# An LSTM with a residual: cutting the input product at whole products, and the order of small jobs at its head

## The chip, the cores and the metric

The kernel runs on one core of a Trainium2 chip. The metric is the time of one execution in device microseconds (us). A core has five engines that matter here. TensorE (PE) multiplies matrices into PSUM; VectorE (DVE) and ScalarE (ACT) do elementwise work; GpSimd (POOL) does a little of it; SyncE (SP) issues most of the transfers (DMAs). Each engine takes its own instructions in the order in which the program wrote them, and waits for others by semaphores. ACT and POOL can issue DMAs too, and then an issue stands in the same queue as their other work.

## What is computed

x has 32 sequences of 512 steps with 512 features, and the result is x plus the hidden states of an LSTM that runs over x:

```python
xW = jnp.einsum('ntd,dg->ntg', x, Wx) + b          # (32, 512, 2048)
def step(carry, xw_t):
    prev_h, prev_c = carry
    a = xw_t + prev_h @ Wh                          # Wh: 512 x 2048
    i = jax.nn.sigmoid(a[:, :Hd])
    f = jax.nn.sigmoid(a[:, Hd:2 * Hd])
    o = jax.nn.sigmoid(a[:, 2 * Hd:3 * Hd])
    g = jnp.tanh(a[:, 3 * Hd:])
    next_c = f * prev_c + i * g
    next_h = o * jnp.tanh(next_c)
    return ((next_h, next_c), next_h)
return x + swapaxes(hs, 0, 1)                       # hs: the 512 hidden states
```

All of it is float32. The product with Wh is serial: step t + 1 needs the hidden state of step t. The product with Wx depends on nothing in the loop, and can be done at any time before its step.

## The kernel before

**Column groups.** A batch of 32 fills 32 of PE's 128 columns. So each product is written as four matmuls, one for each quarter (q or j = 0 to 3) of the output's 128 partitions, and these run in PE's four column groups at the same time. "h" is the product of the hidden state with Wh: 16 matmuls of 512 columns in each step (four for each of four slices k), made by `h_part` (line 201, the matmul is line 210). "x" is the product with Wx. Each matmul shows as two records in the profile, with a weight load for each.

**The x product.** For steps 24 to 503 it is done in 20 groups of 24 steps by a bilinear scheme: 20 slots for each group, of 7 products each (r = 1 to 7), a product being four matmuls of 256 columns on line 477. A group has thus 140 products, 560 matmuls. Its left factors are sums of pieces of x, made by DVE on line 388 (`u_op`) from pair sums (lines 444 to 450) of what `load_group` (line 434) loads. Its right factors are rows of `vring`, loaded by `load_v` (line 556) from a DRAM table `vdram`, three rows ahead. The results are evicted from PSUM by ACT (lines 523, 532, 539) and DVE (lines 529, 533, 536) in `evacuate`, summed by DVE in `w_op` (line 353, 1024 columns), stored to DRAM (line 369), and loaded again by step (`load_xw`, lines 568 and 574).

**One step.** `h_part(t)` is written first, then the stores, loads and elementwise jobs, then the x matmuls (`emit_matmuls`), then `cell(t)`. So the x matmuls fill PE while the cell turns the gates into the next hidden state: ACT's sigmoids and tanh (lines 225 to 227), DVE's products (229, 230), tanh (232), the product with the output gate (234) and two transposes into `ht` (236). On DVE and ACT the jobs of step t stand ahead of `cell(t)`. `seed_step(t + 1)` (line 585) copies the x part of step t + 1 into the PSUM bank onto which `h_part(t + 1)` accumulates. POOL adds x to h for the output (line 244), and SP stores it (line 248).

**How many x matmuls a step gets.** The position `pos` counts x matmuls. In steps from `STREAM0` = 20 on, a step runs up to a target that grows by 560 / 24 = 23.33 matmuls:

```python
target = min(R * 7 * 4 + (t + 1 - STREAM0) * R * 7 * 4 // GS, 4 * len(items))
n = max(0, target - pos[0])
```

Steps thus get 23 or 24 matmuls, and most end inside a product.

**The head, steps 0 to 19.** The x product of the first 24 steps is done plainly (`plain_block`, line 159): five of them before step 0, nineteen in steps 0 to 9, which `keep` (line 715) evicts and stores to DRAM (`kept`, line 716). Meanwhile DVE makes the table of right factors (`v_add`, line 627), and ACT issues its stores (`v_store`, line 639, called by `flush_v`). From step 10 to 19 the stream of group 0 runs, 57 to 59 matmuls in a step (37 in step 19), in chunks of at most 24. After `cell(10)`, ACT issues three loads of bias rows (line 690); `late_seeds` (lines 694 to 704, DVE) makes from them, in step 11, banks' seeds that line 507 copies later. When the plain products and the jobs are over, at the end of step 9, `load_group(1)` is written on SP.

**The tail.** From step 478 on nothing is left of x but eight plain steps, and h alone runs.

Of the kernel before, what the change touches and what calls it, by code (L numbers as in the profile page):

```python
# [23 lines left out]
HEAD = 24  # L24
GS = 24
NG = 20
TAIL = T - HEAD - NG * GS
R = 20
TAU = (1, 0, 2)
NS = NG * R  # L30
KEPT = 5
AHEAD = 28
STREAM0 = HEAD + GS - AHEAD
# [32 lines left out]
PROD = 4 * 108.0  # L66
# [22 lines left out]
def kernel(  # L89
# [10 lines left out]
    nc = tc.nc  # L100
# [35 lines left out]
    def load_x(c, a=0, b=TC):  # L136
        nc.sync.dma_start(
            out=xnat[:, xslot(c), a:b].rearrange("p t q b -> p (t q b)"), in_=x[c][:, a * P : b * P]
        )
# [48 lines left out]
    def is_split(t):  # L188
        return t >= SPLIT

    def bank_of(t):
        if t < KEPT:
            return [gbank[0], gbank[1], xbank[3], xbank[4], xbank[0]][t]
        return gbank[t % 2]

    def half_of(t, i):
        if is_split(t):
            return PAIRS[t % 2][i][:, 0:HW]
        return bank_of(t)[:, i * HW : (i + 1) * HW]
# [234 lines left out]
    def load_group(g):  # L434
        nc.sync.dma_start(
            out=xs[g % 2][:, :, 0:4],
            in_=xg[g].rearrange("p (k s m) -> p k s m", k=6, s=4),
        )
# [14 lines left out]
    items = []  # L453
# [4 lines left out]
    pos = [0]  # L458
# [119 lines left out]
    def seed_step(t):  # L578

        src = xw_late[t] if t in xw_late else xw[:, t % 3]  # L580
        if is_split(t):
            for i in range(2):
                nc.scalar.copy(half_of(t, i), src[:, i * HW : (i + 1) * HW])
        else:
            nc.scalar.copy(bank_of(t), src)  # L585
# [94 lines left out]
    def flush_v():  # L680
        for f in v_stores:
            f()
        v_stores.clear()
# [4 lines left out]
    def load_seeds(pairs, queue):  # L688
        for i, j in pairs:
            queue.dma_start(out=seeds[i], in_=bias[j : j + 1].to_broadcast([P, W]))  # L690
# [21 lines left out]
    def keep(p):  # L712
        n = p - KEPT
        dst = parks[n % 6]
        add(dst, park_banks[n % 3], bias_full)
        kept_stores.append(lambda: nc.sync.dma_start(out=kept[n], in_=dst))

    with tc.manual_schedule():
# [37 lines left out]
        jobs = {}  # L756
# [3 lines left out]
        dve_jobs = []  # L760
# [4 lines left out]
        done_work = 0.0  # L765
        n_plain = 0
        group_loaded = 1
# [9 lines left out]
        for t in range(T):  # L777
            h_part(t)
            for f in stores + kept_stores:
                f()  # L780
            stores.clear()
            kept_stores.clear()
            store_blocks()
            c, rest = divmod(t + 6, TC)
            if rest == 0 and 3 <= c < NCHUNK - 1:
                load_x(c)
            if t == SPLIT - 4:
                load_x(NCHUNK - 1)
            if t == 3:
                load_x(2)  # L790
            if t == 5:
                load_seeds(((4, 3), (5, 1)), nc.sync)
                load_group(0)
            if t + 3 >= KEPT and t + 3 < HEAD + NG * GS and t >= 2:
                if t == 2:
                    pass
                load_xw(t + 3)

            if t < HEAD_STEPS:
                target = head_work * (t + 1) / HEAD_STEPS  # L800
                chunks = []
                while done_work < target - 200 and n_plain < HEAD - KEPT:
                    chunks.append(("plain", KEPT + n_plain))
                    n_plain += 1
                    done_work += PLAIN
                n = int((target - done_work) / PROD * 4 + 0.5) if n_plain == HEAD - KEPT else 0
                if t == HEAD_STEPS - 1 and n:
                    n = R * 7 * 4 - pos[0]
                left = n
                while left > 0:  # L810
                    m = min(left, 24)
                    chunks.append(("stream", m))
                    left -= m
                done_work += n * PROD / 4
                todo = jobs.pop(t, [])
                plains = sum(k == "plain" for k, _ in chunks)
                for i, (kind, m) in enumerate(chunks):
                    if kind == "plain":
                        bank = park_banks[(m - KEPT) % 3]
                        room["dve"] = 3000.0  # L820
                        for cc in range(4):
                            plain_block(m, cc, bank)
                        if i == 0:
                            cell(t)
                            flush_v()
                        keep(m)
                        if m == HEAD - 1:
                            plains_done = t
                        last = i == plains - 1
                        for _ in range(len(todo) if last else -(-len(todo) // (plains - i))):  # L830
                            todo.pop(0)()
                    else:
                        load_v_ahead()
                        u_ahead(m)
                        room["dve"] = m * PROD / 4 * 1.5
                        evacuate()
                        if late_seeds_due and plains_done < t - 1:
                            late_seeds_due.pop()()
                        if t >= HEAD_STEPS - 3 and dve_jobs:
                            dve_jobs.pop(0)()  # L840
                        u_ahead(m + 24)
                        while wqueue and room["dve"] > 0:
                            w_op()
                        seed_banks(m)
                        emit_matmuls(m)
                        if i == 0:
                            cell(t)
                            flush_v()
                            if t == plains_done + 1:
                                load_seeds(((0, 0), (1, 1), (2, 2)), nc.scalar)  # L850
                if t + 1 >= KEPT:
                    seed_step(t + 1)
                if t >= 9 and not v_stores:
                    load_v_ahead()
                if group_loaded == 1 and n_plain == HEAD - KEPT and not dve_jobs and not jobs:
                    assert not v_stores
                    load_group(1)
                    group_loaded = 2
                    dve_jobs += [lambda i=i: pair_sum(1, i) for i in range(4)]
                continue  # L860

            target = min(R * 7 * 4 + (t + 1 - STREAM0) * R * 7 * 4 // GS, 4 * len(items))
            n = max(0, target - pos[0])
            after = max(0, min(R * 7 * 4 + (t + 2 - STREAM0) * R * 7 * 4 // GS, 4 * len(items)) - pos[0])
            room["dve"] = 3800.0 + min(0.0, room["dve"])
            evacuate()
            seed_banks(n)
            if t + 1 < T:  # L870
                seed_step(t + 1)
            load_v_ahead()
            u_ahead(after)
            g_now = items[min(pos[0] // 4, len(items) - 1)][0] // R
            if group_loaded < NG and pos[0] >= 28 * (R * (group_loaded - 1) + 4):
                load_group(group_loaded)
                s_done[group_loaded] = 0
                group_loaded += 1
            g = group_loaded - 1
            if s_done.get(g, 4) < 4 and pos[0] >= 28 * (R * (g - 1) + 9) and room["dve"] > 900:  # L880
                pair_sum(g, s_done[g])
                s_done[g] += 1
            while wqueue and room["dve"] > 300:
                w_op()
            if t == SPLIT - 9:
                late_weights[0] = True
            if t >= SPLIT - 9 and late_loads:
                late_loads.pop(0)()
            emit_matmuls(n)
            kept_late = []  # L890
            for _ in range(0 if t < SPLIT - 2 else 2 if t < SPLIT else 1):
                if plain_tail:
                    p, c = plain_tail.pop(0)
                    plain_block(HEAD + NG * GS + p, c, tail_banks[p % 2])
                    if c == 3:
                        kept_late.append(p)
            cell(t)
            for p in kept_late:
                dst = cbuf[:, take(free_c), 0:2].rearrange("p s c -> p (s c)")
                xw_late[HEAD + NG * GS + p] = dst  # L900
                add(dst, tail_banks[p % 2], bias_full)
            if t == T - 8:
                nc.vector.transpose(x_last, x_of(T - 1).rearrange("p q b -> p (q b)"))
# [50 lines left out]
```

## Time and profile before

| | us |
|---|---|
| median of 3 runs | 3174.75 |
| lowest, highest | 3170.27, 3176.18 |
| the profiled execution's own time | 3174.11 |
| its span, first to last instruction | 3172.0 |
| PE busy on h, L210, into gbank (16288 records) | 1885.6 |
| PE busy on x, L477, into xbank from ubuf (14400 records) | 1209.5 |
| DVE on L353 (480 of 1217 ns) | 580.6 |
| DVE waiting for the gates of ACT (L229 after L226) | 677.3 |
| ACT waiting for h (L225 after L210) | 1283.7 |
| mean granted TensorE clock, share of full | 0.997 |

The profile is of one execution. Busy time counts an engine as busy while at least one of its instructions runs; the matmuls of four column groups overlap, so a busy PE may be a quarter full. A timeline row gives start, duration, engine, line, operation, output and inputs with their shapes, the number of instructions, and in brackets the idle time before the first of them with what ended it. Rows with a q behind the engine (ACTq, SPq) are DMA issues. L585 is line 585 of the kernel before; in the kernel after, the lines from 825 on stand one or two lines further down.

### The profile page before, as it was taken

How to read it: one execution, taken by the hardware profiler on the slowest of the kernel's cores; microseconds unless marked ns; L12 is line 12 of the kernel's file. 1: busy time of each engine (PE TensorE's matmuls, PEld its weight loads, DVE VectorE, ACT ScalarE, POOL GpSimd, SP SyncE). 2: the span in 40 equal slices, each digit the busy share in tenths (PEclk: the TensorE clock that was granted, in tenths of full speed). 3: DMA queues.
4: the chain of work that ended last, by engine and by line, in shares of the span. 5: the costliest groups of instructions: out<-in, count | busy, mean ns of one | idle time of the engine just before them, and what ended most of it. 6: DMA issues, size and time to landing. Idle time of an engine off the chain costs nothing. (4 is left out here: it accounts for less than half of the span.)

```text
span 3172.0 us, 105017 instructions
## 1 busy us (share of the span) xinstructions
PE 3127.2 (99%) x41944; PEld 1999.5 (63%) x41944; DVE 2230.0 (70%) x6217; ACT 1453.0 (46%) x5481; POOL 232.9 (7%) x508
## 2 busy tenths in 40 slices
PE   9899999999999999999999999999999999999998
PEld 6445666666666666666666666666666666666565
DVE  5577767777776777677776767776777767677644
ACT  1144444444444444444444444444444444444444
POOL 0000000000000000000000000000000000000000
PEclk9899999999999999999999999999999999999999
DMA  8877777778778777877778777778777777777831
GB/s 288 291 252 254 249 255 247 249 239 257 254 234 264 227 257 242 262 239 252 243 251 264 226 259 238 255 248 257 241 246 250 252 260 228 251 245 237 269 97 38
DMA packets 311000, 766.66 MB, mean 242 GB/s; under 512 B 49392, under 2 KB 92144, under 8 KB 310000
## 3 DMA queue, kind: packets, MB, share of 16 engines
q1 hardware_dynamic: 296800, 740.82, 72.0%
q10 hardware_dynamic: 13712, 19.14, 1.7%
q8 instruction: 331, 5.42, 0.7%
q14 instruction: 157, 1.29, 0.1%
HBM read 577.04 MB, written 182.71 MB: 240 GB/s over the span
## 5 line engine op out<-in xcount | busy, mean ns | idle before, releaser
L210 PE MATMUL gbank<-wh_sb,ht 128*32 128x512 f32 (+1 forms) x16288 | 1885.6, 580 | 20.1 <-ACT gbank L585 5.5
L210 PEld LDWEIGHTS gbank<-wh_sb,ht 128*32 128x32 f32 x16288 | 843.4, 110 | 684.0 <-issue 311.1
L477 PE MATMUL xbank<-vring,ubuf 128*32 128x256 f32 x14400 | 1209.5, 379 | 8.7 <-DVE cbuf L533 5.2
L477 PEld LDWEIGHTS xbank<-vring,ubuf 128*32 128x32 f32 x14400 | 734.7, 110 | 261.9 <-issue 35.8
L225 ACT ACTIVATE s<-gbank 128x128 f32<-128x128 f32 x984 | 276.3, 281 | 1307.9 <-PE gbank L210 1283.7
L229 DVE TENSOR_TENSOR prod<-s 128x128 f32<-128x128 f32 x1024 | 293.2, 286 | 679.0 <-ACT s L226 677.3
L353 DVE TENSOR_TENSOR cbuf<-cbuf 128x1024 f32<-128x1024 f32 x480 | 580.6, 1217 | 3.3
L244 POOL TENSOR_TENSOR oc<-xnat,ht 128x128 f32<-128x128 f32 x504 | 232.7, 462 | 2901.5 <-DVE ht L236 1603.3
L232 ACT ACTIVATE tanh_c<-s 128x64 f32<-128x64 f32 x1024 | 262.2, 256 | 264.3 <-DVE s L230 260.4
L477 PE MATMUL bbank<-vring,ubuf 128*32 128x256 f32 x2400 | 306.6, 380 | 1.6 <-DVE cbuf L529 1.5
L236 DVE STREAM_TRANSPOSE ht<-hbuf 128x64 f32<-128x64 f32 x1022 | 250.9, 245 | 75.9 <-DVE hbuf L234 2.8
L585 ACT COPY gbank<-xw 128x512 f32<-128x512 f32 x473 | 284.8, 602 | 20.9 <-issue 8.4
L230 DVE TENSOR_TENSOR s<-prod 128x64 f32<-128x64 f32 x1024 | 230.3, 225 | 35.2
L523 ACT COPY cbuf<-xbank 128x512 f32<-128x512 f32 x400 | 233.3, 583 | 44.7 <-PE xbank L477 33.8
L477 PE MATMUL xbank<-vring,r 128*32 128x256 f32 x2400 | 247.5, 379 | 0.4 <-ACT xbank L507 0.4
L477 PE MATMUL xbank<-vring,xs 128*32 128x256 f32 x2400 | 241.8, 381 | 3.3 <-DMA vring<-vdram 3.3
L234 DVE TENSOR_TENSOR hbuf<-o,tanh_c 128x64 f32<-128x64 f32 x1024 | 211.9, 207 | 26.0 <-ACT tanh_c L232 25.4
L226 ACT ACTIVATE s<-gbank 128x64 f32<-128x64 f32 x984 | 228.2, 232 | 0.0
L533 DVE TENSOR_TENSOR cbuf<-xbank,cbuf 128x256 f32<-128x256 f32 x400 | 163.6, 409 | 79.3 <-ACT cbuf L532 76.8
L477 PEld LDWEIGHTS bbank<-vring,ubuf 128*32 128x32 f32 x2400 | 141.7, 110 | 57.1 <-issue 30.0
L529 DVE TENSOR_TENSOR cbuf<-bbank,cbuf 128x256 f32<-128x256 f32 x400 | 161.8, 405 | 4.3 <-PE bbank L477 4.3
L536 DVE TENSOR_TENSOR cbuf<-xbank,cbuf 128x256 f32<-128x256 f32 x400 | 162.3, 406 | 0.4 <-PE xbank L477 0.4
(83 smaller groups left out, 1778.6 us busy)
## 6 DMA issues: line engine op xcount, KB each, us to landing
vring<-vdram SPq DMA_DIRECT2D x340, 896.0 KB, 5.9
xwd<-cbuf SPq DMA_DIRECT2D x240, 512.0 KB, 6.4
xw<-xwd SPq DMA_DIRECT2D x1920, 64.0 KB, 3.6
out_dram<-oc SPq DMA_DIRECT2D x255, 128.0 KB, 2.9
xnat<-in_x_dram SPq DMA_DIRECT2D x63, 512.0 KB, 5.2
xs<-in_x_grouped_dram SPq DMA_DIRECT2D x10, 1536.0 KB, 10.3
vring<-vdram SPq DMA_DIRECT2D x20, 768.0 KB, 6.0
r<-in_x_grouped_dram SPq DMA_DIRECT2D x10, 1536.0 KB, 10.6
```

The lines of the kernel that those rows point to most:

```text
L210: nc.tensor.matmul(dst[j * B : (j + 1) * B], state["ht"][:, k], m, start=False, stop=True, skip_group_check=True)
L225: nc.scalar.activation(s[:, u, 0:2], g[:, n_, 0:2], AF.Sigmoid)
L226: nc.scalar.activation(s[:, u, 2], g[:, n_, 3], AF.Tanh)
L229: nc.vector.tensor_mul(prod[:, u], s[:, u, 0:2], s[:, u, 2:4])
L230: add(nxt[:, u, 3], prod[:, u, 0], prod[:, u, 1])
L232: nc.scalar.activation(tanh_c[:, HALVES[u]], nxt[:, u, 3], AF.Tanh)
L236: nc.vector.transpose(ht[:, 2 * u : 2 * u + 2].rearrange("p q b -> p (q b)"), hbuf[:, HALVES[u]])
L244: (nc.gpsimd if t < T - 8 else nc.vector).tensor_add(oc[:, tt % 2], x_of(t), ht)
L353: op(c_of(dst), c_of(src), c_of(bb))
L477: nc.tensor.matmul(dst[q * B : (q + 1) * B], left_of(gr, s, r)[:, q * B : (q + 1) * B], vring[:, row % 3, RIGHT[r]], start=start, stop=Tru ...
L523: nc.scalar.copy(t[:, 0:4:3], xb.rearrange("p (n c) -> p n c", n=2))
L585: nc.scalar.copy(bank_of(t), src)
```

## The change

Three things change, all in the order of the program; no arithmetic does.

1. The number of x matmuls in a step is rounded to a multiple of four, in the head (to the nearest) and in the stream (the target is rounded down to a whole product). In the stream the steps get 20 or 24 matmuls, one in six 20.
2. In the head `seed_step(t + 1)` moves from the end of the step to directly behind `cell(t)`, ahead of `flush_v`: on ACT the copy of line 585 then precedes the DMA issues of line 639 and the evictions of the later chunks.
3. The three bias loads of step 10 are issued by GpSimd in place of ScalarE, and `load_group(1)` waits for the end of step 13.

```diff
-                n = int((target - done_work) / PROD * 4 + 0.5) if n_plain == HEAD - KEPT else 0
+                n = 4 * int((target - done_work) / PROD + 0.5) if n_plain == HEAD - KEPT else 0
...
                         if i == 0:
                             cell(t)
+                            if t + 1 >= KEPT:
+                                seed_step(t + 1)
                             flush_v()
                         keep(m)
...
                         if i == 0:
                             cell(t)
+                            seed_step(t + 1)
                             flush_v()
                             if t == plains_done + 1:
-                                load_seeds(((0, 0), (1, 1), (2, 2)), nc.scalar)
-                if t + 1 >= KEPT:
-                    seed_step(t + 1)
+                                load_seeds(((0, 0), (1, 1), (2, 2)), nc.gpsimd)
                 if t >= 9 and not v_stores:
                     load_v_ahead()
-                if group_loaded == 1 and n_plain == HEAD - KEPT and not dve_jobs and not jobs:
+                if t >= 13 and group_loaded == 1 and n_plain == HEAD - KEPT and not dve_jobs and not jobs:
                     assert not v_stores
                     load_group(1)
...
-            target = min(R * 7 * 4 + (t + 1 - STREAM0) * R * 7 * 4 // GS, 4 * len(items))
+            target = min(R * 7 * 4 + (t + 1 - STREAM0) * R * 7 // GS * 4, 4 * len(items))
             n = max(0, target - pos[0])
-            after = max(0, min(R * 7 * 4 + (t + 2 - STREAM0) * R * 7 * 4 // GS, 4 * len(items)) - pos[0])
+            after = max(0, min(R * 7 * 4 + (t + 2 - STREAM0) * R * 7 // GS * 4, 4 * len(items)) - pos[0])
```

`after` is how far DVE prepares left factors ahead. With it, and with the chunks of the head, some instructions of lines 388 and 353 move by a step: in the head the program gives step 11 one L388 fewer ahead of the L694s and step 14 one more, and step 20 one L353 more; in the stream, single L388 and L353 move between neighbouring steps.

## The prediction

> **What bounds the kernel now.** I read the page's part 1, then the timeline step by step, then the stretches of the head.
>
> ```profile
> PE 3127.2 (99%) x41944; PEld 1999.5 (63%) x41944; DVE 2230.0 (70%) x6217; ACT 1453.0 (46%) x5481; POOL 232.9 (7%) x508
> ```
>
> PE at 99% says little: a matmul here fills one of four column groups of 32, so PE counts as busy while three groups idle. I therefore measure steps from gate to gate, a gate being the start of a step's first L225 (it follows the last h matmul). Within a group, h matmuls follow each other at 858 ns (two records, 429 apart), x matmuls at 432 (two, 216 apart). A step with six x matmuls in a group lasts 4 x 858 + 6 x 432 = 6024 ns, and the gates show 6023 or 6024 in five steps of six. The sixth is ruled by the cell: t = 71 lasts from gate 560.00 to 565.78, 5780 ns, though five x matmuls need 5592. Per six steps each group gets 35 products, so five in one step; with cut products the groups take that short step at different times, and only when the last has had it does the gate come early. So today's short step falls on t = 5 mod 6, and there DVE often misses it. Here is such a step, t = 101:
>
> ```profile
> 737.02 0.24 DVE L236 STREAM_TRANSPOSE ht<-hbuf 128x64 f32<-128x64 f32 x1
> 737.36 0.39 ACT L532 COPY cbuf<-xbank 128x256 f32<-128x256 f32 x1
> 737.78 0.43 DVE L533 TENSOR_TENSOR cbuf<-xbank,cbuf 128x256 f32<-128x256 f32 x1 [0.51 <-ACT cbuf L532]
> 738.45 1.08 DVE L388 TENSOR_TENSOR ubuf<-xs 128x896 f32<-128x896 f32 x1
> 739.45 2.48 DVE L353 TENSOR_TENSOR cbuf<-cbuf 128x1024 f32<-128x1024 f32 x2
> 740.97 0.28 ACT L225 ACTIVATE s<-gbank 128x128 f32<-128x128 f32 x1 [2.73 <-PE gbank L210]
> 741.85 0.28 DVE L229 TENSOR_TENSOR prod<-s 128x128 f32<-128x128 f32 x1
> 743.10 0.25 DVE L236 STREAM_TRANSPOSE ht<-hbuf 128x64 f32<-128x64 f32 x1
> 743.47 0.19 PEld L210 LDWEIGHTS gbank<-wh_sb,ht 128*32 128x32 f32 x8 [0.69 <-ACT cbuf L539]
> ```
>
> The gate is at 740.97 and L229 should follow 0.43 later, as elsewhere (710.85 to 711.27); it starts at 741.85, 0.46 late, because DVE still runs L388 and two L353 behind an eviction that waited 0.51 for ACT. h starts late by that; the step lasts 6228, 448 over 5780. By position (t mod 24; the pattern of products repeats every 24 steps) the medians are 6228 (5), 6095 (11), 6228 (17), 5780 (23); all others 6024.
>
> The head (to 270 us) has two real holes:
>
> ```profile
> 86.19 3.19 ACTq L639 DMA_DIRECT2D vdram<-vring  x4
> 89.42 0.59 ACT L585 COPY gbank<-xw 128x512 f32<-128x512 f32 x1 [2.99 <-issue]
> 90.06 6.59 PE L210 MATMUL gbank<-wh_sb,ht 128*32 128x512 f32 x32 [4.91 <-ACT gbank L585]
> ...
> 138.94 0.55 SPq L435 DMA_DIRECT2D r<-in_x_grouped_dram  x1
> 142.74 4.45 ACTq L690 DMA_DIRECT2D r<-in_L_cond_b_dram  x3
> 147.24 0.37 ACT L532 COPY cbuf<-xbank 128x256 f32<-128x256 f32 x1 [4.24 <-DMA r<-in_x_grouped_dram]
> 148.12 1.08 PE L477 MATMUL xbank<-vring,ubuf 128*32 128x256 f32 x8 [4.43 <-DVE cbuf L533]
> 153.38 1.93 PE L477 MATMUL xbank<-vring,xs 128*32 128x256 f32 x16 [3.33 <-DMA vring<-vdram]
> ```
>
> ACT issues DMAs (L639, L690) while a seed or an eviction waits behind them. After each hole the granted clock is low (PEclk, third from the end, in the windows view):
>
> ```profile
> 92.00:100.00 8.00, 8.00 (x91) 3.66 (x85) 1.68 (x8) 1.36 (x7) 0.45 (x1) 0.75 0.46 170
> 150.00:160.00 10.00, 6.67 (x60) 2.57 (x60) 5.59 (x9) 0.58 (x1) 0.00 (x0) 0.63 0.76 307
> 230.00:240.00 10.00, 7.88 (x131) 4.61 (x126) 9.07 (x19) 4.21 (x14) 0.46 (x1) 1.00 0.37 125
> ```
>
> Holes of 4.91 and 4.43 us cost clock; the third stretch holds a hole of 2.12 at full clock.
>
> **The change, part by part.** The sum is made on the profiled execution: 3174.11 us (span 3172.0), 0.64 under the median 3174.75.
>
> *Whole products, steps 26 to 473.* Per step 23, 23, 24 become 20, 24, 24, 24, 24, 24: at every step's end the new position is the old one rounded down to a whole product, so the same products are finished in each step, and evictions keep their steps. Six-product steps stay 6024. The short step is now short for all groups at once, at t = 2 mod 6, and costs 5780 by the row of t = 71 (not 5592: the cell rules it). That alone gives nothing, one short step in six as before. What changes is where DVE's heavy steps fall. Positions 5, 11 and 17 now have six products, in which ht has 6024 - 5780 = 244 ns to spare; the same DVE queues overrun by 448 - 244 = 204, 315 - 244 = 71 and 204. The new short steps (2, 8, 14, 20) queue on DVE three evictions and two larger operations, in lone durations 3.38 to 3.65 us (three of 0.41; two of 0.94 to 1.22), with at most 0.1 of waiting, since L532 is ACT's first there. The room is 4.12: from the last transpose (gate + 2.33) to the next L229 (6.02 + 0.43). No overrun. Position 19 gets three L353 (4.46 in lone durations, some 4.2 back to back), hidden in the 244. Per 24 steps: before 1215 of overrun on today's short steps, after 479 on long ones, and 244 x 3 = 732 is gained. Counted step by step over 26 to 473: 2689.5 against the measured 2704.1 (scattered irregular steps included, taken as staying). **-14.0 us**, bounds -14.6 and 0.
>
> *Seed copy ahead of the stores.* In step 5 tanh ends on ACT at 86.44; the copy (0.59) ends at 87.03 instead of 90.01, the first transpose ended at 86.63, so h starts at 87.08: -2.98. The hole shrinks to 1.9 us, less than the 2.12 that kept the clock, so the h part takes 3.64 instead of 6.59: -2.95. The stores it passes then issue 0.6 later; nobody reads them within 30 us. In step 9 h starts 0.6 earlier, worth nothing: x then waits for L388 (first x at 138.74 in any case). **-5.9**, bounds -5.9 and -3.0 (clock drops all the same).
>
> *Bias loads off ACT, group load to step 13 or later.* In old times: ACT's L532 can run at 143.6 (seed copy 0.6 first) instead of 147.24, PE's hole ends near 144.5 and not 148.12. Row 3 of vring was issued at 142.09, behind the group load, on which SP stood until 138.94, and landed for 153.38; without the group load it issues when row 0 is done (139.7), takes the median 5.9 and lands at 145.6, when PE gets there. So h(11) starts near 146.3 at full clock: gate 11 at 150.0 instead of 160.45. **-10.4**, of which 0.5 is five matmuls put off.
>
> *What it costs.* (a) The L694s in step 11 now precede the L388 for slot 4 on DVE (before, one L388 stood ahead of them), and PE needs it after six products, at 152.3. No trace shows a DMA issued by GpSimd. Nearest rows: L690 landed 7.9 (median) after issue, and 12.0 from first issue to the last L694. Counted from GpSimd's free time, 144.2, plus 4.2 of DVE work, L388 ends at 156.3 or 160.4: a stall of 4.0 or 8.1; 0 if they land like xw (3.6). I take 3, below the middle row, since the group load no longer shares the engines. GpSimd's next add and the out store on SP behind it come 10 us later. (b) The group load now meets vring rows at step 14: +1, 0 to 3 (3.33 was such a wait). (c) Step 14 gets an L388 more and one eviction fewer on a full DVE: +0.5. (d) Step 20 gets a fourth L353 and a fourth eviction (7.57 of work against 5.95) and only 20 matmuls to hide it: +1.5. (e) The put-off matmuls: +0.5.
>
> Head: -5.9 - 10.4 + 3 + 1 + 0.5 + 1.5 + 0.5 = **-10**. Whole: 3174.1 - 14 - 10 = **3150**, -0.8%.
>
> [...]
>
> **Rivals.** *The slack isn't there:* the heavy steps pay 448, 315, 448 on top of 6024, as if h could not absorb a late ht. For it: every overrun in the trace is paid in full. Against: those are the steps without slack. Time 3174.1 - 10 = 3164. *The late bias eats the head:* (a) at 8.1, with the hole over 4.4 us and a clock drop of 3 more: +8; time 3158. *The new short steps become DVE bound* (slower): if their queue overran as t = 101 does, each of 75 short steps would cost 448, 33.6 us; time 3184. It outweighs the gains from 0.32 us per short step, a queue of some 4.4 us with its waits. Against: my count is 3.75 at most.
>
> **How the numbers follow.** Forecast 0.62 (3142 to 3158), better than it 0.07, late bias 0.15, no slack 0.10, slower 0.06. The range reaches over the late bias and most of the third: 3139 to 3165. 0.2% (6.3 us, about what a measurement can tell from no change) puts the line at 3168: faster 0.89, same 0.05, slower 0.06.
>
> **What would show it.** Gates 5780 at t = 2 mod 6; 6228, 6095, 6228 at positions 5, 11, 17 unchanged although six products now run there; no short step on 5 mod 6; L585 ahead of L639 near 86.4 and clock 1.00 in 92:100; no L690 on ACT; a wait of PE for L388 in step 11. Wrong if short steps exceed 5800, if L694 waits over 8 us, or if vring waits appear after the moved group load.

## The result, and the profile after

The changed kernel takes 3151.13 us (median of 4, 3150.15 to 3154.46), the kernel before 3175.47 beside it (median of 4, 3170.27 to 3178.71): a ratio of 0.9927, 95% interval 0.991 to 0.9944. The forecast was 3150. The profiled execution took 3150.15, its span is 3148.0, 24.0 less than before, and the mean granted clock is 0.999. The first part of its page:

```profile
PE 3119.0 (99%) x41944; PEld 1616.1 (51%) x41944; DVE 2232.8 (71%) x6217; ACT 1454.6 (46%) x5481; POOL 235.6 (7%) x511
```

The counts of instructions are those of before but for POOL's three more; busy time says as little as it did. What counts are the gates, taken as in the prediction from the first L225 of each step:

| stage, after less before | predicted | measured |
|---|---|---|
| step 5 | -5.9 | -6.05 |
| step 9 | 0 | +1.55 |
| step 10 | -10.4 | -11.09 |
| step 11 | +3 | +8.38 |
| steps 12 to 19 | +2 | -3.32 |
| steps 20 to 25 | +1.5 | +1.18 |
| steps 26 to 473 | -14.0 | -13.43 |
| step 474, at the turn to the tail | 0 | -1.19 |

(Before step 0 another 0.60 is gained, and behind step 474 0.57 is lost again; the steps of the head that aren't listed are within 0.01.) The steady part is as forecast: medians of 5779 ns at t = 2, 8, 14, 20 mod 24, 6234, 6100, 6234 at positions 5, 11, 17, and 6023 or 6024 at all others, 5 mod 6 no more short. Here is t = 101 again, in the timeline after:

```profile
725.38 0.42 DVE L533 TENSOR_TENSOR cbuf<-xbank,cbuf 128x256 f32<-128x256 f32 x1 [0.51 <-ACT cbuf L532]
...
726.05 1.08 DVE L388 TENSOR_TENSOR ubuf<-xs 128x896 f32<-128x896 f32 x1
727.05 2.48 DVE L353 TENSOR_TENSOR cbuf<-cbuf 128x1024 f32<-128x1024 f32 x2
728.56 0.28 ACT L225 ACTIVATE s<-gbank 128x128 f32<-128x128 f32 x1 [2.72 <-PE gbank L210]
729.45 0.28 DVE L229 TENSOR_TENSOR prod<-s 128x128 f32<-128x128 f32 x1
...
734.79 0.28 ACT L225 ACTIVATE s<-gbank 128x128 f32<-128x128 f32 x1 [2.48 <-PE gbank L210]
```

The same queue in the same order, the same wait of 0.51, and L229 again 0.46 late. Yet the step holds six products now and still lasts 6.23: the lateness costs 0.2 over a step of 6.02, where it had cost 0.45 over one of 5.78.

The two holes of the head in the timeline after (ACTq rows are issues by ACT; L690 on POOL is the issue by GpSimd):

```profile
85.74 0.58 ACT L585 COPY gbank<-xw 128x512 f32<-128x512 f32 x1
85.99 2.90 ACTq L639 DMA_DIRECT2D vdram<-vring  x3
86.37 3.64 PE L210 MATMUL gbank<-wh_sb,ht 128*32 128x512 f32 x32 [1.82 <-ACT gbank L585]
...
135.19 1.07 ACT L523 COPY cbuf<-xbank 128x512 f32<-128x512 f32 x2 [4.54 <-DMA vdram<-cbuf]
...
139.20 1.75 POOL L690 DMA_DIRECT2D r<-in_L_cond_b_dram  x3
...
143.72 0.43 DVE L694 TENSOR_TENSOR r<-r 128x256 f32<-128x256 f32 x1 [2.97 <-DMA r<-in_L_cond_b_dram]
146.60 0.43 DVE L694 TENSOR_TENSOR r<-r 128x256 f32<-128x256 f32 x1 [2.46 <-DMA r<-in_L_cond_b_dram]
148.46 0.42 DVE L694 TENSOR_TENSOR r<-r 128x256 f32<-128x256 f32 x1 [1.43 <-DMA r<-in_L_cond_b_dram]
150.85 1.08 DVE L388 TENSOR_TENSOR ubuf<-xs 128x896 f32<-128x896 f32 x1
151.86 0.28 DVE L229 TENSOR_TENSOR prod<-s 128x128 f32<-128x128 f32 x1
151.99 1.94 PE L477 MATMUL xbank<-vring,ubuf 128*32 128x256 f32 x16 [5.27 <-DVE ubuf L388]
```

The copy stands ahead of the stores, and PE waits 1.82 in place of 4.91. The hole of step 10 is gone. A new one has come in step 11: L694 waits three times for the biases, L388 and the cell's L229 stand behind it, and PE waits 5.27. The windows view (PEclk is third from the end):

```profile
92.00:100.00 8.00, 8.00 (x125) 5.47 (x117) 5.94 (x11) 0.35 (x1) 0.46 (x1) 1.00 1.03 386
150.00:160.00 10.00, 7.73 (x88) 3.23 (x92) 7.75 (x19) 3.88 (x10) 0.45 (x1) 0.67 0.17 54
```

Full clock after the hole of 1.82, and 0.67 in the ten us after that of 5.27. By the clock records of the trace the clock is 0.50 from 149.68 to 156.50, and PE works again from 151.99: 4.5 us at half clock, which lose about 2.3 (an estimate). Between its gates step 11 also runs one product more (60 matmuls against 56), worth 0.43: without the hole, in e6 below, it takes 9.91, and before the change 9.48. With the hole of 5.27 this makes 8.0 of the 8.38 by which step 11 is longer.

### The profile page after: what moved, and what is told of

Read it like the earlier page. It is cut to its first block, busy times and chain, and to the rows that moved or that the text cites. A ratio compares the mean times of both kernels' runs of the same rounds, so it can differ in the third digit from the quotient of the medians.

```text
span 3148.0 us, 105007 instructions
## 1 busy us (share of the span) xinstructions
PE 3119.0 (99%) x41944; PEld 1616.1 (51%) x41944; DVE 2232.8 (71%) x6217; ACT 1454.6 (46%) x5481; POOL 235.6 (7%) x511
## 3 DMA queue, kind: packets, MB, share of 16 engines
q14 instruction: 157, 1.29, 0.1%
## 4 chain that ended last, share of the span: by engine, by line
PE 94%; DVE 3%; DMA 2%; issue 1%; ACT 1%; SPq 0%; POOL 0%; DVEq 0%; ACTq 0%; POOLq 0%
PE gbank L210 52%; PE xbank L477 31%; PE bbank L477 5%; PE xbank L159 2%; PE xbank L210 2%; DVE cbuf L353 1%; PE bbank L159 1%; DMA r<-in_L_cond_Wx_dram 0%; DMA xw<-xwd 0%; DMA xs<-in_L_cond_Wx_dram 0%; DVE prod L229 0%; DVE ubuf L388 0%; DMA vring<-vdram 0%; DVE s L230 0%; DMA r<-in_L_cond_b_dram 0%
## 5 line engine op out<-in xcount | busy, mean ns | idle before, releaser
L210 PE MATMUL gbank<-wh_sb,ht 128*32 128x512 f32 (+1 forms) x16288 | 1792.7, 579 | 6.9 <-DVE ht L236 2.3
L210 PEld LDWEIGHTS gbank<-wh_sb,ht 128*32 128x32 f32 x16288 | 615.0, 110 | 905.7 <-issue 727.1
L477 PE MATMUL xbank<-vring,ubuf 128*32 128x256 f32 x14400 | 932.8, 379 | 10.7 <-DVE ubuf L388 5.9
L225 ACT ACTIVATE s<-gbank 128x128 f32<-128x128 f32 x984 | 275.9, 281 | 1291.5 <-PE gbank L210 1270.9
L477 PEld LDWEIGHTS xbank<-vring,ubuf 128*32 128x32 f32 x14400 | 560.7, 110 | 377.0 <-issue 179.1
L229 DVE TENSOR_TENSOR prod<-s 128x128 f32<-128x128 f32 x1024 | 293.8, 287 | 648.6 <-ACT s L226 648.1
L353 DVE TENSOR_TENSOR cbuf<-cbuf 128x1024 f32<-128x1024 f32 x480 | 581.2, 1218 | 3.9
L523 ACT COPY cbuf<-xbank 128x512 f32<-128x512 f32 x400 | 233.8, 585 | 40.8 <-PE xbank L477 27.2
L533 DVE TENSOR_TENSOR cbuf<-xbank,cbuf 128x256 f32<-128x256 f32 x400 | 164.0, 410 | 79.0 <-ACT cbuf L532 74.8
L477 PE MATMUL bbank<-vring,ubuf 128*32 128x256 f32 x2400 | 192.3, 379 | 0.6 <-DVE cbuf L529 0.6
L477 PE MATMUL xbank<-vring,xs 128*32 128x256 f32 x2400 | 172.3, 381 | 0.8 <-DVE cbuf L533 0.5
L477 PE MATMUL xbank<-vring,r 128*32 128x256 f32 x2400 | 171.6, 379 | 0.1
L529 DVE TENSOR_TENSOR cbuf<-bbank,cbuf 128x256 f32<-128x256 f32 x400 | 162.0, 405 | 2.7 <-PE bbank L477 2.7
L539 ACT COPY cbuf<-xbank 128x256 f32<-128x256 f32 x400 | 145.3, 363 | 20.4 <-PE xbank L477 11.1
```

The costliest lines, as they stand in the source:

```text
L210: nc.tensor.matmul(dst[j * B : (j + 1) * B], state["ht"][:, k], m, start=False, stop=True, skip_group_check=True)
L225: nc.scalar.activation(s[:, u, 0:2], g[:, n_, 0:2], AF.Sigmoid)
L229: nc.vector.tensor_mul(prod[:, u], s[:, u, 0:2], s[:, u, 2:4])
L353: op(c_of(dst), c_of(src), c_of(bb))
L477: nc.tensor.matmul(dst[q * B : (q + 1) * B], left_of(gr, s, r)[:, q * B : (q + 1) * B], vring[:, row % 3, RIGHT[r]], start=start, stop=Tru ...
L523: nc.scalar.copy(t[:, 0:4:3], xb.rearrange("p (n c) -> p n c", n=2))
```

## The experiments

All ratios are against the kernel before, which ran beside each group of four on the same chip: 3175.15 (e1 to e4), 3175.57 (e5 to e8) and 3176.81 (e9 to e12). Two things move single times by some us whatever the kernel: the gate of step 0 stood between 29.4 and 33.0 us, and step 474 lasted between 8.8 and 12.8. So medians are compared for the whole, and gates stage by stage for causes.

**The two halves.** e1 is the kernel before with the two lines of the stream's target changed; e2 is the changed kernel with those two lines as before.

> The kernel before with the whole products of steps 20 to 511 alone; head untouched. Theory (slack: a late ht is absorbed by 244 ns where six products run): steps at t = 2, 8, 14, 20 mod 24 at 5780 ns, positions 5, 11, 17 at 6228, 6095, 6228, all others 6024; -13 to -15 us, so 3161 to 3163, ratio 0.9955. Rival (the head alone made the gain, the gates only look better because the step is counted elsewhere): 3173 to 3177, ratio 1.000.

> The changed kernel with the old rounding in steps 20 to 511: the head's edits alone. Theory: step 5 at 8.9 us instead of 15.0, step 10 about 11 shorter, step 11 about 8 longer, positions 5, 11, 17, 23 of the steady part as in the kernel before (6228, 6095, 6228, 5780); -9 to -11 us, so 3164 to 3166, ratio 0.9968. Rival (the gains of head and steady part are not independent, the head's edits shift transfers of the steady part): anything 2 us away from the remainder of the other run, that is, the two gains do not add up to 24.

e1: 3161.56, 0.996 (0.9947 to 0.9974), with the medians named and 12.6 us less in steps 26 to 473. e2: 3166.63, 0.997 (0.9959 to 0.9982); step 5 takes 8.94, step 10 11.1 less, step 11 8.9 more, and positions 5, 11, 17, 23 are 6233, 6100, 6233, 5781. That is 13.6 and 8.5, in sum 22.1 of the 24.3; the rest is within the intervals. The two halves are independent as far as can be measured, and the larger one is the stream.

**Where the short step falls.** Only the phase of the rounding is changed.

```diff
-            target = min(R * 7 * 4 + (t + 1 - STREAM0) * R * 7 // GS * 4, 4 * len(items))
+            target = min(R * 7 * 4 + ((t + 1 - STREAM0) * R * 7 + 5 * GS // 6) // GS * 4, 4 * len(items))
```

(and the same in the next line; e4 has 2 for 5).

> The changed kernel with 5/6 of a product added to the position before it is rounded: the short step falls on t = 1 mod 6 and DVE's second products sit in other steps. From the program's order and lone durations (L533 0.41, L536 0.41, L529 0.41, L388 1.08, L353 1.22, L444/446/448 0.94) positions 5, 11, 17 have 3.5, 3.4, 3.5 us of DVE work after the cell instead of 4.33, 4.20, 4.33; the new short steps have 1.9 (1), 4.19 (7), 0.8 (13), 4.33 (19). Slack theory: a queue that begins with L533 may hold 4.125 us in a step of six products and 3.881 in a short one (4.329 less 0.204, 4.197 less 0.071); one that begins with L529 or L536 waits for no ACT copy and may hold at least 4.218 in a short step (4.462 ran without overrun in a six-product step, less 0.244). So the 204, 71, 204 go, and at most 0.110 comes at position 19: 369 to 479 ns less per 24 steps, -6.9 to -8.9 us against the changed kernel: 3142 to 3144. Rival (alignment: the gain is that all column groups end a product together, wherever the short step falls): 3151, as the changed kernel.

> The changed kernel with 2/6 of a product added before rounding: the short step falls on t = 4 mod 6. By the program's order DVE's queues are 4.33 at positions 5 and 17 (six products), 4.60 at position 10 (533 536 529 448 353 353, a short step), 3.52 at 4, 16 and 22 (short). Slack theory: 204 at 5 and 17, and 4.602 - 3.881 = 721 at position 10 (a step of 6.50 us), in all 1129 ns per 24 steps against 479 in the changed kernel: +12 us, 3163. Rival (alignment, wherever the short step falls): 3151.

e3: 3149.27, 0.9916 (0.9902 to 0.9929). e4: 3156.8, 0.9936 (0.9923 to 0.9948). Against the changed kernel's profile their steps 26 to 473 are 2.5 shorter and 5.3 longer. (By its whole time alone e3 can't be told from the changed kernel; the gates show the difference.) Whole products alone don't set the time, then: it depends on which DVE queues meet the short step, and that ends the rival. But both sizes were off by more than half. In e3, 5, 11 and 17 went to 6023 as expected, and 7 and 19 take 5909 and 6045, so 129 and 265 ns of overrun, not 0 to 110. In e4, 5 and 17 take 6204, not 6228, and 10 takes 6226, not 6501. The limits of 4.125 and 3.881 were taken from one sort of queue. The timeline of e3, from the queue behind the cell at position 6, and of e4, behind the cell at position 4:

```profile
737.84 0.37 ACT L532 COPY cbuf<-xbank 128x256 f32<-128x256 f32 x1
...
738.24 0.42 DVE L533 TENSOR_TENSOR cbuf<-xbank,cbuf 128x256 f32<-128x256 f32 x1 [0.36 <-ACT cbuf L532]
```

```profile
723.93 0.38 ACT L532 COPY cbuf<-xbank 128x256 f32<-128x256 f32 x1
...
724.34 0.42 DVE L533 TENSOR_TENSOR cbuf<-xbank,cbuf 128x256 f32<-128x256 f32 x1 [0.24 <-ACT cbuf L532]
```

In e4 ACT has one copy ahead of L532 (L523), and L533 waits 0.24; in the changed kernel it has two (L539, L523), and L533 waits 0.51. In e3 L529 goes first, but L533 behind it still waits 0.36 for ACT. So DVE's room in a step isn't one number: ACT's order comes off it. With 0.27 less waiting the expectation's own sums give e4's sizes: 4.602 - (4.125 + 0.27) + 0.244 for the short step is 0.451 us at position 10 (0.446 measured; L533 waits 0.24 there too), and 4.329 - (4.125 + 0.27) + 0.244 for the short step ahead of it is 0.178 at position 5 (0.180 measured).

**No long queue at all.** One number of the changed kernel is changed; the sum L353 is put off to a neighbouring step when a step's room is small.

```diff
-            while wqueue and room["dve"] > 300:
+            while wqueue and room["dve"] > 1200:
```

> The changed kernel with one number changed: a second or third sum (L353) is put on DVE in a step only while the step's room is over 1200 instead of 300. By the program's order no DVE queue of the steady part is then above 3.66 us (before 4.33, 4.20, 4.33 at positions 5, 11, 17 and 4.46 at 19); the sums put off go to steps 13 and 18. Slack theory: positions 5, 11, 17 at 6024, the short ones stay 5780, and the 204, 71, 204 that the changed kernel still pays per 24 steps are gone: -8.9 us over the steady part, 3142. Rival (h is late at these positions for another reason, L533's wait of 0.51 for ACT alone): 0.51 exceeds the 0.244 of slack by 0.27 whatever follows it, so nothing goes: 3151.

e5: 3142.13, 0.9892 (0.9877 to 0.9907). Every position is at 6023 or 6024 but the four short ones at 5779, and steps 26 to 473 are 8.8 shorter. Its t = 101:

```profile
724.86 0.43 DVE L533 TENSOR_TENSOR cbuf<-xbank,cbuf 128x256 f32<-128x256 f32 x1 [0.51 <-ACT cbuf L532]
...
726.53 1.22 DVE L353 TENSOR_TENSOR cbuf<-cbuf 128x1024 f32<-128x1024 f32 x1
728.05 0.28 ACT L225 ACTIVATE s<-gbank 128x128 f32<-128x128 f32 x1 [2.73 <-PE gbank L210]
728.47 0.29 DVE L229 TENSOR_TENSOR prod<-s 128x128 f32<-128x128 f32 x1 [0.72 <-ACT s L226]
```

The wait of 0.51 is still there, one L353 has gone, and L229 comes 0.42 after the gate. The rival falls: the wait alone is paid by nobody. The overrun was the whole queue, and the slack theory had its size to 0.2 us here (8.9 expected).

**The biases in step 11.** In e6 only the operations on them move; the loads stay where they are.

```diff
-                        if late_seeds_due and plains_done < t - 1:
+                        if late_seeds_due and plains_done < t - 2:
```

> The changed kernel with the six operations on the biases (L694, L702 to L704) one step later, in step 12. Theory (in step 11 L388, and behind it the cell's L229, stand on DVE behind L694s that wait for the biases' landing): PE's wait of 5.27 for L388 in step 11 goes and the clock stays 1.00 in the 10 us after it; step 11 takes about 9.5 instead of 17.9, step 12 at most 1 to 2 more for 3.4 us of DVE work: -6.5 us, 3144 to 3146. Rival (behind the biases the next thing is as late: the vring row or xs that PE needs): step 11 above 14, less than 3 us gained: 3148 to 3151.

e6: 3146.18, 0.9902 (0.9888 to 0.9916), 5 us under the changed kernel. Step 11 takes 9.91 in place of 17.86, and step 12 9.42, as before: the late operations cost nothing there. In its timeline L388 runs as soon as its evictions are done, and the three L694 follow ten us later with no wait between them:

```profile
143.59 1.08 DVE L388 TENSOR_TENSOR ubuf<-xs 128x896 f32<-128x896 f32 x1
...
154.33 1.09 DVE L694 TENSOR_TENSOR r<-r 128x256 f32<-128x256 f32 x3
```

So the new hole was nothing but the order on DVE: a wait for a transfer ahead of what PE needs next. Of the 7.95 that step 11 loses, the median keeps 5; in this profile (3148.73, the longest of the four) steps 9 and 10 take 1.65 more, with a hole of 2.21 and a fall of the clock, and step 474 3.4 more.

**The group load and the queue of the biases.** e7 takes `t >= 13 and` away; e10 gives the bias loads back to ACT (`nc.gpsimd` becomes `nc.scalar`). Both are the changed kernel otherwise.

> The changed kernel without the condition t >= 13: the group load (L435) is issued after step 9 as before the change. Theory: SP stands on it until its room is free, so the two kept stores (L716), which in the changed kernel run beside the vdram stores of step 9 (DMA share 1.00 to 1.03 between 125 and 135 us), come after them again; L523's wait for the vdram store in step 9 is shorter, step 9 takes 13.4 or 13.5 instead of 14.95; but row 3 of vring is issued behind the group load and lands late, as before the change, which adds 0 to 3 us to step 10 or 11 (how much is hidden beneath the wait for the biases is open): 3150 to 3153. Rival (the 1.5 us in step 9 come from the seed copy ahead of the stores): step 9 stays at 14.9.

> The changed kernel with the three bias loads issued by ACT again, everything else kept. Theory (the queue matters little as long as step 11 waits for the landing): ACT stands 4.45 us on L690 and PE waits about as long in step 10, but the biases land at about the same time, so PE's 5.27 us of waiting for L388 in step 11 shrink by as much; steps 10 and 11 together stay within 2 us of 25.96, unless the clock falls a second time: 3151 to 3153. Rival (ACT's 4.45 us are paid on the path whatever comes after, as the ledger of the prediction has it): steps 10 and 11 together at 30, 3155 to 3156.

e7: 3157.18, 0.9936 (0.9924 to 0.9949). In the timeline of its steps 9 and 10:

```profile
131.90 0.56 SPq L435 DMA_DIRECT2D r<-in_x_grouped_dram  x1
...
133.26 0.58 ACT L523 COPY cbuf<-xbank 128x512 f32<-128x512 f32 x1 [2.60 <-PE xbank L477]
...
146.21 1.08 PE L477 MATMUL xbank<-vring,xs 128*32 128x256 f32 x8 [7.46 <-DMA vring<-vdram]
```

Step 9 takes 13.43 again; L523 no longer waits for the vdram store (4.54 above). The last kept stores are issued after the group load, at 133.19, and in the changed kernel from 125.32 on, between the vdram stores. In all four profiles with the early group load step 9 takes 13.4 to 14.0, in the other ten 14.3 to 16.9. That the stores share the DMA engines (share 1.00 to 1.03 there) is the likely reason, and only argued. And the late row of vring costs PE 7.46, more than the 3.33 before the change. In this execution that replaces the hole of step 11 (steps 9 to 11 take 41.06, in the changed kernel 40.91), but the median is 6 higher, twice the upper end expected; where the other executions lose it, no profile of theirs shows.

e10: 3150.38, 0.9915 (0.9902 to 0.9929), as the changed kernel. Its L690 on ACT, which took 4.45 before the change:

```profile
139.94 0.38 ACTq L690 DMA_DIRECT2D r<-in_L_cond_b_dram  x1
...
140.37 0.93 ACTq L690 DMA_DIRECT2D r<-in_L_cond_b_dram  x2
```

It takes 1.31. Steps 10 and 11 together take 21.08 here, against 25.96; the biases land sooner than in the changed kernel's profile (the last L694 at 146.72, 6.8 after the first issue, against 9.3; the other profiles with GpSimd's issue and the same order have 7.1 to 9.0). The medians show no difference between the two queues. The rival, that ACT's 4.45 is paid, is refuted, and so is the theory's own reason, that ACT stands 4.45 and something hides it: it doesn't stand. In e8 below, with the group load early and the loads on ACT, L690 takes 0.39 + 4.25. What held ACT stands in the traces. First the kernel before, then e8:

```profile
146.86 0.33 ACTq L690 DMA_DIRECT2D r<-in_L_cond_b_dram  x1
147.24 0.37 ACT L532 COPY cbuf<-xbank 128x256 f32<-128x256 f32 x1 [4.24 <-DMA r<-in_x_grouped_dram]
```

```profile
142.13 0.33 ACTq L690 DMA_DIRECT2D r<-in_L_cond_b_dram  x1
142.51 0.37 ACT L532 COPY cbuf<-xbank 128x256 f32<-128x256 f32 x1 [3.98 <-DMA r<-in_x_grouped_dram]
```

Only the third of the three loads is late, and the idle time ahead of L532 is ended by the group load. In the trace of the kernel before, that third issue has the same semaphore as the group load (104) and waits on it: the group load's last landing is at 146.84 and the issue at 146.86 (e1: 146.05 and 146.07; e8: 142.11 and 142.13). In e10, with the group load late, it waits for nothing. So ACT stood on a wait for another transfer's landing, not on slow issuing. Either move alone frees it: the group load's (e10) or the queue's (e7, whose L532 runs without idle time before it while the group load is in flight).

**The seed copy alone, and the head's rounding alone taken back.** e8 is the kernel before with only part 2 of the change; e9 is the changed kernel with this line as before:

```diff
-                n = 4 * int((target - done_work) / PROD + 0.5) if n_plain == HEAD - KEPT else 0
+                n = int((target - done_work) / PROD * 4 + 0.5) if n_plain == HEAD - KEPT else 0
```

> The kernel before with the seed copy put ahead of the stores alone. Theory: step 5 at 8.94 instead of 14.99, step 9 unchanged or 0.6 shorter than 13.4 (the group load still stands ahead of the kept stores), step 10 0.6 shorter at most, all others as before: -6 to -7 us, 3168 to 3169. Rival (the seed copy delays the vdram stores and so L523 in step 9): step 9 at 14.9, 1.5 us less gained: 3170.5.

> The changed kernel with the old rounding in steps 10 to 19 of the head alone (products cut between steps as before the change). Theory: the seed copy now stands ahead of L532 in these steps, and where cut products leave DVE late as well (in the kernel with the seed copy alone, steps 12 to 19 take 84.2 us in sum, 78.9 in the changed kernel, and 83.2 before), L529 comes late for PE; so steps 12 to 19 go from 78.9 to about 84, step 20 from 6.92 to 6.02: +4 to +5 us, 3155 to 3156. Rival (the gain of 4.4 us in steps 12 to 19 comes from the loads moved off ACT or the later group load): steps 12 to 19 stay at 79, 3151.

e8: 3173.87 (median of 11), 0.9995 (0.9986 to 1.0003): next to nothing. Step 5 gives its 6.05. Step 9 then takes 0.55 more, step 10 1.29 more, and steps 12 to 19 2.0 more, so that at gate 26, counted from gate 0, only 2.1 is left. The timeline around step 18 shows how, first before the change and then in e8:

```profile
223.60 0.42 DVE L533 TENSOR_TENSOR cbuf<-xbank,cbuf 128x256 f32<-128x256 f32 x1 [0.16 <-ACT cbuf L532]
...
227.75 0.64 PE L477 MATMUL bbank<-vring,ubuf 128*32 128x256 f32 x8 [1.02 <-DVE cbuf L529]
```

```profile
219.46 0.58 ACT L585 COPY gbank<-xw 128x512 f32<-128x512 f32 x1
...
221.12 0.42 DVE L533 TENSOR_TENSOR cbuf<-xbank,cbuf 128x256 f32<-128x256 f32 x1 [0.68 <-ACT cbuf L532]
...
225.27 0.64 PE L477 MATMUL bbank<-vring,ubuf 128*32 128x256 f32 x8 [1.27 <-DVE cbuf L529]
```

The seed copy now stands ahead of the step's evictions on ACT; L533 waits 0.52 longer, DVE, busy 9.32 of the ten us from 220 on, passes it on, and PE waits 0.25 longer for L529 at this place. Over the whole run PE's waits for L529 go from 3.6 to 4.6, which is half of the 2.0; the other half isn't traced.

e9: 3160.49, 0.995 (0.9937 to 0.9962). Steps 12 to 19 take 84.9 in place of 78.9, as expected; the median rose by 9, twice the 4 to 5, of which steps 20 to 25 give back 1.2 and steps 9 and 10 add 1.4. What the waits view of PE says of L529 in the changed kernel, and in e9 (total, times, longest):

```profile
PE bbank L477 <- DVE cbuf L529: 0.6, 2, 0.4
```

```profile
PE bbank L477 <- DVE cbuf L529: 4.6, 4, 2.6
```

The rounding in the head, priced at +0.5, thus gains some 5 us (6.1 in steps 12 to 19, less 1.2 in steps 20 to 25), and 4.0 of waits for L529 go with it. That is shown; that a cut product asks for its bank a step earlier than DVE can clear it is the likely reason, and only argued.

**What the experiments point to.**

> The changed kernel with both changes that gained: sums put on DVE only while the room is over 1200, and the operations on the biases in step 12. Theory: the two act in different steps (steady part, head) and add up: -9 and -5 against the changed kernel, 3136 to 3138. Rival (the sums put off fill DVE in the head, where the late operations now stand): less than 3 of the 5 remains, 3139 to 3142.

> The changed kernel with sums put on DVE only while the room is over 1200, and the three bias loads issued by GpSimd at the end of step 9 instead of step 10, as soon as their room is free; their operations stay in step 11. Theory (only the landing is late): they land some 10 us earlier, L694 in step 11 waits for nothing, step 11 takes 9.4 to 9.9: 3136 to 3138. Rival (in step 9 the DMA engines are full, share 1.00 to 1.03 between 125 and 135 us in the changed kernel, and the loads take from the stores of vdram, for which L523 waits there): step 9 and 10 together rise by more than 3 us over 23.1: 3140 to 3142.

e11 (both lines of e5 and e6): 3137.12, 0.9875 (0.9862 to 0.9889), 40 us under the kernel before and 14 under the changed one; the two gains add up. e12 (the room of e5; the loads of biases at the end of step 9, the operations in step 11 as in the changed kernel): 3143.19, 0.9897 (0.9882 to 0.9912). Its step 11 takes 9.91 as hoped, but steps 9 and 10 take 27.1 (23.1 in the changed kernel, 22.4 in e11). Its windows view, DMA share second from the end:

```profile
130.00:140.00 10.00, 5.63 (x68) 2.35 (x64) 4.92 (x7) 1.57 (x4) 1.11 (x3) 0.93 1.04 365
```

and its timeline in that stretch:

```profile
139.02 1.07 ACT L523 COPY cbuf<-xbank 128x512 f32<-128x512 f32 x2 [6.46 <-DMA vdram<-cbuf]
...
139.66 3.64 PE L477 MATMUL xbank<-vring,ubuf 128*32 128x256 f32 x32 [3.72 <-ACT cbuf L523]
```

PE waits 3.72 for L523 there, and L523 6.46 (4.54 in the changed kernel) for the vdram store. That is what the rival said, but it isn't shown to be the loads' doing: e5, which differs from e12 only in that the loads stand in step 10, has 25.2 in steps 9 and 10 and a wait of 5.34 at L523, so 1.8 and 1.1 are left for them, by one execution of each. What the medians show is that the early issue gained nothing over e5 (3143.19 and 3142.13), while the late operations of e11 gained 5. Here the way to hide a late transfer was to ask for it later, not to issue it earlier.

## Why the prediction was right, point by point

*Whole products* (-14.0, measured -13.43): right in mechanism, places and size. e1 gives it alone, and e3, e4 and e5 show that it is the meeting of DVE's queues with the short step, not the whole product as such. Of the 0.6 that lacks, 0.2 lies in scattered irregular steps (0.9 over the regular pattern before, 1.2 after). The rest was in the forecast: 732 ns per 24 steps make 13.7 over these steps, and the count that gave 14.6 seems to set steps without irregular ones against a sum that has them. (The overrun before adds up to 1211, not 1215.) The rival that the slack isn't there is out: 6234, 6100 and 6234 are some 240 under what it would give (448, 315 and 448 over 6024).

*Seed copy* (-5.9, measured -6.05 in step 5): right there, clock included; the yardstick, a hole of 2.12 at full clock, is one case (behind 2.16 the clock fell in e4 and not in e3, see the last section), and behind 1.82 it stayed at 1.00. But "in step 9 h starts 0.6 earlier, worth nothing" left out that from step 10 on the copy passes the evictions too. The prediction listed what it passes in step 5 and not in the later steps. Alone it brings 1.7 (interval around nothing), as e8 shows.

*Bias loads and group load* (-10.4, measured -11.09 in step 10): the sum was right and its cause half wrong. What failed is the reading of L690's 4.45 as time that the issues themselves take ("ACT issues DMAs (L639, L690) while a seed or an eviction waits behind them"): without the group load they take 1.31 on ACT, and e10, which leaves them there, is as fast. ACT waited for the group load's landing, and the row of L532 in the prediction names it (`4.24 <-DMA r<-in_x_grouped_dram`). The move to GpSimd wasn't needed once the group load was late. The group load's move also has a cost that was put at nothing: kept stores are now issued between the vdram stores, and step 9 takes 1.55 more (e7 takes it back).

*The costs.* (a) The late biases were put at 3, with rows at 0, 4.0 and 8.1; step 11 takes 8.4 more. The stall itself is 5.27, which is about the upper row less the 2.7 by which the last L694 came sooner (9.3 after the first issue, against 12.0 before). So the discount "since the group load no longer shares the engines" had the right sign (the biases landed after 6.7 us, median, and after 9.0 in e7, beside the group load) and was too large. The fall of the clock behind the hole, some 2.3, was kept for the rival and belongs to this term. (b) No wait for vring is found at step 14, nothing in place of 1. With (c) and (e), steps 12 to 19 were to be 2 longer and are 3.3 shorter. The term that failed is (e): to the head's rounding the prediction gave nothing but its put-off matmuls (0.43 of them are found in step 11), and it gains some 5 (e9) and pays for the seed copy's 2 there. (d) 1.5, measured 1.18 for steps 20 to 25; with the even queues of e5 step 20 takes 5.79 and the 1.18 is gone.

The head came to -9.36 in place of -10 because two errors met: 5.4 too little cost in step 11, 5.3 too much in steps 12 to 19. That they cancel was luck. The total was right to 1.1 us; the ledger of the head was not.

## What to carry to other kernels

Rate a step by what it can absorb, not only by how much is queued in it: an overrun costs only what exceeds the slack, so short steps go where the helping engine's queue is short, or the queue is made even (9 us here by one number). An engine that seems to stand on a DMA issue may be waiting for another transfer to land; see what ended its idle time before moving the one that is seen to wait. When an instruction is moved forward, list what it passes in every step that has it, and keep a wait for a transfer behind what the bottleneck needs next.

## What was not expected of the hardware

The same three loads of 256 KB, issued by GpSimd in 1.75 us, took between 4.9 (e6) and 7.1 us (e11; median to landing) in the eight kernels that issue them in step 10 and have the group load late, and 9.0 in e7, with the group load beside them. Where, of the eight, their operations stand in step 11, that step lasted 13.6 to 18.4 us. The issues of three such loads by ACT took 1.31 us where none of them had to wait for the group load (e10); most of the 4.45 (before), 3.98 (e1) and 4.64 (e8) was that wait.

The clock: holes of PE of 1.82 (the changed kernel), 1.95 (e10) and 2.12 us (the kernel before) left it at 1.00, one of 2.21 (e6) was followed by some 3.4 us at 0.50. In windows of ten, the one of 5.27 showed as 0.67, that of 7.46 (e7) as 0.66. In these runs a hole's length alone didn't tell whether the clock fell: PE's wait for L523 in step 9 is 2.16 long in e4 and in e3, and the clock falls in e4 alone (the 32 matmuls behind the wait take 3.55 us there, 1.93 in e3); holes of 2.37 and 2.6 in e9 left it at 1.00. Here are two stretches of 3.41 us around that wait, in e4 (its hole from 134.93 to 137.09) and in e3 (135.11 to 137.28):

```profile
133.82:137.23 3.41, 1.25 (x28) 0.53 (x20) 0.12 (x1) 0.78 (x2) 0.00 (x0) 1.00 0.89 290
137.23:140.65 3.42, 3.42 (x36) 1.76 (x35) 2.10 (x9) 2.35 (x10) 0.62 (x2) 0.50 0.51 155
```

```profile
132.79:136.21 3.42, 1.93 (x32) 0.94 (x32) 1.34 (x2) 0.00 (x0) 0.00 (x0) 1.00 0.94 297
136.21:139.62 3.41, 2.35 (x44) 1.46 (x48) 1.40 (x7) 2.62 (x10) 0.00 (x0) 1.00 0.90 280
```

In e4 PE idles 2.16 us of the first stretch, and the second is at 0.50. In e3 the same wait is shared by the two, which idle 1.49 and 1.06 us, and both are at 1.00. Whether that sharing made the difference, one pair of runs doesn't show. In the clock records of the two kernels the clock is at 0.50 for 6.83 and 10.24 us before, with 51.20 at 1.00 between them, and for 6.83 us after (a last stretch that runs past the end of the work aside): 2, 3, 15 and 2 times 3.41.
